# The end of the second layer of a two-layer selective-scan kernel: earlier loads, spread norm sums and a hand-ordered tail

## The chip, the cores and the metric

The kernel runs on one core of one Trainium2 chip. The metric is the device time of one execution in microseconds (us); lower is better. Of the kernel before the change three runs are shown, and their median is 1526.66 us (1522.29 to 1531.98).

## What is computed

Two layers work on an image x of 64 x 64 positions with 96 channels. Each adds a block to x: a group norm, a projection to 192 channels and 192 gate channels, a 3 x 3 convolution per channel with SiLU, a selective scan over the positions in four directions, the sum y of the four results, a layer norm over the 192 channels, the product with SiLU of the gates, and a projection back to 96 channels. The change is in the last steps of layer 2:

```python
y = out_y[:, 0] + out_y[:, 1, :, ::-1] + out_y[:, 2][:, :, i1] + out_y[:, 3][:, :, i2]
...
mu = y.mean(-1, keepdims=True)
var = y.var(-1, keepdims=True)
y = (y - mu) * lax.rsqrt(var + LN_EPS) * ln_gamma + ln_beta
y = y * jax.nn.silu(z)
return y @ out_proj_w.T
```

## The kernel before

**Layout.** The 192 channels of half the positions each lie in three tiles `y[T]`, T = 0, 1, 2, of 128 partitions by 2048 columns: 64 partitions for one half of the positions, 64 for the other. The columns are worked on in four chunks c of 512. x itself lies transposed, `xT`, 96 partitions by 4096 positions; two half chunks h of 512 positions belong to each c. In DRAM lie x (`xs`) and the gates after SiLU (`szd`), both written earlier.

**The scans of layer 2** (`scans`, from L839) are 16 groups (direction and chunk) of 24 units. A unit is one block T and one pair m of states: ScalarE makes the decay `a`, TensorE the input `b`, VectorE scans them to `h` (two units cost one product `b<-b,du` and two scans), GpSimd multiplies by C (`hc`), TensorE sums into `ys`. The order on every engine is written out by hand: in unit j a loop issues stage_B or stage_t, a, b, r, s, k, y and c for units near j, and then the extra steps whose slot has come. The extra steps of a group's prelude prepare the next group; those of `early_norms` (L1180) run in the last group. They do the layer norm of chunks 3, 2 and 1, which are complete by then: per chunk three matmuls for the mean (`em`), a copy, three subtractions on GpSimd, three squares on ScalarE, three matmuls for the variance (`ev`), and the reciprocal root into `u[0]`. Chunk 0 is completed by the last group itself. In each chunk the three matmuls of a sum fall into one unit.

**Pools.** `pre` holds the scan's tiles that live once, `mn` those with several buffers; `tail` opens after both are closed, and its tiles take over their memory. A new tile waits for the last use of the tiles that it lies on. The memory is given out in the order in which tiles are first asked for. In the kernel before, `xT` (16 KB per partition) and the gate tiles `szt` lie on scan tiles up to the last group's `du`, `su` and `B3`.

**The tail of layer 2** (`tail`, L1490) has no fixed order; a scheduler orders each engine's instructions. All twelve gate tiles and four pieces of `xT` are loaded on SP's queue (L1505, L1507). `centre(0)` and `scale(0)` do the norm of chunk 0 (L1514 to L1529). Then for c = 3, 2, 1, 0: `gated` multiplies and shifts y and multiplies by the gates (L1538 and L1541 on VectorE; for T = 2 of chunks 3, 2 and 1 L1543 to L1545 on GpSimd and ScalarE), `project` does six matmuls into `o` (L1552) and two additions into `xT` (L1558), and `tokens` transposes back (L1569), copies (L1571) and sends the result (L1572), with a single PSUM buffer `t`.

Of the kernel before, what the change touches and what calls it, by code (L numbers as in the profile page):

```python
# [19 lines left out]
DM = 96  # L20
DI = 192
NS = 16
NP = NS // 2
RK = 6
TC = 1024
HT = TC // 2
NCH = L // TC
# [5 lines left out]
NB = 96  # L33
# [4 lines left out]
V_CW, V_CB, V_G, V_B, V_D = 0, 9, 10, 11, 12  # L38
NV = 16

HALF = (slice(0, 64), slice(64, 128))
# [3 lines left out]
def two_ss2d_layers(  # L45
# [46 lines left out]
    ident = const.tile([128, 128], F32, name="ident")  # L92
    make_identity(nc, ident)

    pos = const.tile([128, 128], F32, name="pos")
# [10 lines left out]
    for h in range(2):  # L106
        t = const.tile([128, 128], F32, name=f"wide{h}")
# [10 lines left out]
    eps5 = const.tile([128, 1], F32, name="eps5")  # L118
# [25 lines left out]

    u = [pers.tile([128, L // 2], F32, name=f"u{T}") for T in range(3)]
    y = [pers.tile([128, L // 2], F32, name=f"y{T}") for T in range(3)]
    xs = dpool.tile([DM, L], F32, name="xs")
    szd = [dpool.tile([3, 128, L // 2], F32, name=f"szd{l}") for l in range(2)]

# [2 lines left out]
    xT = xp.enter_context(tc.tile_pool(name="xT0", bufs=1)).tile([DM, L], F32, name="xT0")  # L152
    st = [pers.tile([DM, 8, 6], F32, name=f"st{l}") for l in range(2)]
    with tc.tile_pool(name="ld", bufs=8) as ld, tc.tile_pool(
        name="ldp", bufs=4, space=PSUM
# [682 lines left out]
    def scans(weights):  # L838
# [18 lines left out]
        with ExitStack() as sc:  # L857
# [2 lines left out]
            pps = sc.enter_context(tc.tile_pool(name="pps", bufs=1, space=PSUM, reuse_waits="tile"))  # L860
            dram = sc.enter_context(tc.tile_pool(name="dram", bufs=3, space=DRAM))
            am = []
            carry = pre.tile([128, 3, NP], F32, name="carry")
            PER = 3 * NP
            LAG = 3
            halves = [slice(0, HT), slice(HT, TC)]
# [1 line left out]

            xd = pre.tile([128, TC], F32, name="xd")
            dve.memset(xd[96:128], 1.0)  # L870

            def spare(name, tag="v"):

# [304 lines left out]
            def early_norms():  # L1178


                steps = []
                squares = [chunk(u[T], 0) for T in range(3)]
                for c, at, lead, end in ((3, 2, 0, 8), (2, 8, 2.1, 14), (1, 14, 10, 20)):
                    me, mean = {}, chunk(u[1], c)

                    def average(me, c, of, T, what):
                        if T == 0:
                            me[what] = spare(f"{what}{c}")
                        pe.matmul(me[what], pos, of[T], start=(T == 0), stop=(T == 2))

                    def keep(me, mean):
                        act.copy(mean, me["em"])

                    def centre(T, c, mean):
                        pool.tensor_sub(chunk(y[T], c), chunk(y[T], c), mean)

                    def square(T, c):
                        act.activation(squares[T], chunk(y[T], c), AF.Square)

                    def root(me, c):  # L1200
                        act.activation(chunk(u[0], c), me["ev"], AF.Ln, bias=eps5)
                        act.activation(chunk(u[0], c), chunk(u[0], c), AF.Exp, scale=-0.5)

                    of = [chunk(y[T], c) for T in range(3)]
                    for T in range(3):
                        steps += [
                            (lead + 0.35 * T, partial(average, me, c, of, T, "em")),
                            (at + 2 * T, partial(centre, T, c, mean)),
                            (at + 2 * T + 1.5, partial(square, T, c)),
                            (end + 0.35 * T, partial(average, me, c, squares, T, "ev")),  # L1210
                        ]
                    steps += [(lead + 1.1, partial(keep, me, mean)), (end + 1.4, partial(root, me, c))]
                return [(PER * (len(GROUPS) - 1) + at, step) for at, step in steps]

            units = [
# [274 lines left out]

    def tail(l, w, xT):


        op, v = w["op"], w["v"]
        with ExitStack() as sc:
# [14 lines left out]
            def centre(c):  # L1510
                cut = slice(HT * c, HT * (c + 1))
                pm = fps.tile([128, HT], F32, tag="m", name=f"m_{l}_{c}")
                for T in range(3):
                    nc.tensor.matmul(pm, pos, y[T][:, cut], start=(T == 0), stop=(T == 2))  # L1514
                for T in range(3):
                    nc.vector.tensor_sub(y[T][:, cut], y[T][:, cut], pm)
                    sq = live[c, T] = fin.tile([128, HT], F32, tag=f"sq{T}", name=f"sq{l}_{c}_{T}")
                    nc.scalar.activation(sq, y[T][:, cut], AF.Square)

            def scale(c):  # L1520
                cut = slice(HT * c, HT * (c + 1))
                pv = fps.tile([128, HT], F32, tag="v", name=f"v_{l}_{c}", bufs=1)
                for T in range(3):
                    nc.tensor.matmul(pv, pos, live[c, T], start=(T == 0), stop=(T == 2))
                rstd = live[c] = fin.tile([128, HT], F32, tag="rstd", name=f"rstd{l}_{c}")
                if c == order[0] and not l:
                    load_exp_ln()
                nc.scalar.activation(rstd, pv, AF.Ln, bias=eps5)
                nc.scalar.activation(rstd, rstd, AF.Exp, scale=-0.5)  # L1529

            def gated(c):
                cut = slice(HT * c, HT * (c + 1))
                rstd = live.pop(c) if c in live else u[0][:, cut]
                for T in range(3):
                    q = live[c, T] = fin.tile([128, HT], F32, tag=f"g{T}", name=f"g{l}_{c}_{T}")
                    gain, bias = v[:, T, V_G : V_G + 1], v[:, T, V_B : V_B + 1]
                    if l == 0 or T < 2 or c == 0:
                        nc.vector.scalar_tensor_tensor(  # L1538
                            q, y[T][:, cut], gain, rstd, ALU.mult, ALU.mult
                        )  # L1540
                        nc.vector.scalar_tensor_tensor(q, q, bias, sz[c, T], ALU.add, ALU.mult)  # L1541
                    else:
                        nc.gpsimd.tensor_mul(q, y[T][:, cut], rstd)  # L1543
                        nc.scalar.activation(q, q, AF.Identity, bias=bias, scale=gain)
                        nc.gpsimd.tensor_mul(q, q, sz[c, T])  # L1545

            def project(c):
                gs = [live.pop((c, T)) for T in range(3)]
                po = fps.tile([DM, 2, HT], F32, tag="o", name=f"o{l}_{c}")
                for T in range(3):  # L1550
                    for h, half in enumerate(HALF):
                        nc.tensor.matmul(  # L1552
                            po[:, h], op[half, T, :], gs[T][half], start=(T == 0), stop=(T == 2)
                        )
                for h in range(2):
                    g = 2 * c + h
                    cut = slice(g * 512, (g + 1) * 512)
                    nc.vector.tensor_add(xT[:, cut], po[:, h], xT[:, cut])  # L1558
                    if l == 0:
                        nc.vector.bn_stats(w["next"][:, g, :], xT[:, cut])  # L1560
                        nc.sync.dma_start(out=xs[:, cut], in_=xT[:, cut])

            def tokens(c):

                for g in (2 * c, 2 * c + 1):
                    pt = fps.tile([128, 4, DM], F32, tag="t", name=f"t{l}_{g}", bufs=1)
                    for j in range(4):
                        t = slice(g * 512 + 128 * j, g * 512 + 128 * (j + 1))
                        nc.tensor.transpose(pt[:, j], xT[:, t], ident[0:DM, 0:DM])  # L1569
                    ob = fin.tile([128, 4, DM], F32, tag="ob", name=f"ob{g}")  # L1570
                    nc.scalar.copy(ob, pt)  # L1571
                    nc.sync.dma_start(  # L1572
                        out=out[g * 512 : (g + 1) * 512, :].rearrange("(j p) c -> p j c", p=128),
                        in_=ob,
                    )

            if l:
                centre(0)
                scale(0)
                for c in order:  # L1580
                    gated(c)
                    project(c)
                    tokens(c)
                return
            steps = (centre, lambda c: (scale(c), gated(c)), project)
            for i in range(NCH + len(steps) - 1):
                for lag, step in enumerate(steps):
                    if 0 <= i - lag < NCH:
                        step(order[i - lag])

    for l in range(2):

# [108 lines left out]
```

## Time and profile before

| | us |
|---|---|
| median of three runs | 1526.66 |
| the profiled execution | 1525.39 |
| its span | 1523.6 |
| busy in the span: VectorE, TensorE, ScalarE, GpSimd | 1353.6, 1242.7, 1214.6, 1120.0 |
| last scan `h` ends | 1479.73 |
| first load of the tail issued | 1479.76 |
| last copy `ob` ends | 1520.05 |

Times in the profile are us from the start of the span. A timeline line gives start, busy time, engine, line, operation, what is written and read, and how many instructions are merged in it; in brackets stands the idle time of the engine ahead of it and what ended it. L852 is the line of the helper that records all instructions of the scans, so that there one goes by tile names. Of each 512-column fp32 matmul the trace holds two records. `SPq` is the sequencer that issues DMAs.

### The profile page before, as it was taken

Reading aid. Unit: us, or ns where it says so; the run is one execution under the profiler, and the core shown is the slowest. Engines: PE = TensorE matmul, PEld = TensorE weight load, DVE = VectorE, ACT = ScalarE, POOL = GpSimd, SP = SyncE. Lnnn points to the kernel's source line nnn. Section 1 sums busy time; section 2 is a strip of 40 time slices with the busy share of each in tenths; the row PEclk is TensorE's granted clock in tenths of the full one; section 3 lists DMA queues with packets and bytes.
Section 4 is the critical chain, followed back from the end, with each engine's and each line's share of the span. In section 5 each row is a group of like instructions: output and inputs, shape, how many; then the busy total and the mean of one; then the engine's idle time right before and its main releaser. Section 6 shows DMA issues by size and latency. Waiting matters only on the chain.

```text
span 1523.6 us, 17338 instructions
## 1 busy us (share of the span) xinstructions
PE 1242.7 (82%) x5122; PEld 499.9 (33%) x5122; DVE 1353.6 (89%) x945; ACT 1214.6 (80%) x2498; POOL 1120.0 (74%) x608
## 2 busy tenths in 40 slices
PE   6944879688788888889788888797988888876986
PEld 3323433233232323333333333333333233322332
DVE  5956579579999999999999999999999999999985
ACT  6573355679998989898999889989898989887852
POOL 0023000369999898989898989898989899899991
PEclk9965889579998999999999999999989998999998
DMA  3230512514352626162626262626353444535324
GB/s 110 78 88 2 136 42 83 126 30 111 85 133 64 147 62 154 56 140 56 140 57 139 58 139 60 149 68 141 75 122 86 110 101 94 121 75 132 77 59 134
DMA packets 79796, 146.33 MB, mean 96 GB/s; under 512 B 27676, under 2 KB 30940, under 8 KB 79596
## 3 DMA queue, kind: packets, MB, share of 16 engines
q1 hardware_dynamic: 78540, 142.78, 38.7%
q0 software_dynamic: 576, 1.57, 0.4%
q8 instruction: 42, 0.69, 0.2%
q10 hardware_dynamic: 576, 0.79, 0.2%
q14 instruction: 62, 0.51, 0.1%
HBM read 80.85 MB, written 12.13 MB: 61 GB/s over the span
## 4 chain that ended last, share of the span: by engine, by line
DVE 29%; issue 21%; PE 13%; ACT 8%; DMA 6%; POOL 6%; SPq 5%; DVEq 0%; POOLq 0%; ACTq 0%
DVE h L852 16%; DVE b L852 7%; POOL hc L852 4%; SPq L852 4%; PE ys L852 4%; DMA cb<-C 3%; ACT a L852 3%; DVE acc L1468 3%; PE b L852 3%; PE pj L852 2%; ACT bT L852 2%; DMA du<-su 2%; DMA szt<-szd 2%; PE pd L852 1%; PE o L1552 1%
## 5 line engine op out<-in xcount | busy, mean ns | idle before, releaser
L852 POOL TENSOR_TENSOR hc<-h,cb 128x1024 f32<-128x1024 f32 x384 | 903.2, 2367 | 109.0 <-DVE h L852 60.2
L852 DVE TENSOR_TENSOR_SCAN h<-a,carry,b 128x1024 f32<-128x1024 f32 x288 | 664.9, 2337 | 30.1 <-PE b L852 7.2
L852 ACT ACTIVATE a<-dt,am 128x1024 f32<-128x1024 f32 x384 | 438.5, 1142 | 92.6 <-DVE h L852 87.4
L852 PE MATMUL ys<-hc,fold 128*64 128x512 f32 x1536 | 430.1, 640 | 2.8 <-POOL hc L852 2.8
L852 ACT ACTIVATE bT<-duT,BT 128x192 f32<-128x192 f32 x1012 | 386.9, 445 | 6.5 <-PE b L852 4.5
L852 PE MATMUL b<-ident,bT 128*128 128x128 f32 x1536 | 223.3, 289 | 30.7 <-DVE h L852 24.2
L852 DVE TENSOR_TENSOR b<-b,du 128x1024 f32<-128x1024 f32 x192 | 232.3, 1210 | 14.8 <-PE b L852 14.6
L852 DVE TENSOR_TENSOR_SCAN h<-a,b 128x1024 f32<-128x1024 f32 x96 | 216.0, 2277 | 15.1 <-PE b L852 4.5
L852 PEld LDWEIGHTS b<-ident,bT 128*128 128x128 f32 x1536 | 176.2, 147 | 156.6 <-DVE h L852 91.5
L852 PE MATMUL b<-B,selh 96*128 96x512 bf16 x384 | 122.7, 403 | 84.2 <-DVE h L852 84.2
L852 PEld LDWEIGHTS ys<-hc,fold 128*64 128x64 f32 x1536 | 78.4, 139 | 139.8 <-issue 98.5
L852 PE MATMUL pj<-u,xw 64*124 64x512 f32 x192 | 97.9, 656 | 5.2 <-ACT sz L1425 2.0
L852 PE MATMUL pd<-xd,dwb 29*64 29x512 f32 x192 | 61.1, 714 | 47.8 <-DVE w L852 41.1
L852 PEld LDWEIGHTS <-selh 96*128 96x128 bf16 x384 | 26.4, 98 | 213.8 <-DVE h L852 114.5
L1468 DVE SCALAR_TENSOR_TENSOR acc<-pad,v,acc 128x1052 f32<-128x1052 f32 (+1 forms) x80 | 91.3, 1200 | 0.6
L852 POOL DMA_DIRECT2D du<-su x12 | 6.4, 538 | 83.0 <-DVE am L237 80.5
L852 PE MATMUL ys<-y,ident 128*128 128x512 f32 (+1 forms) x120 | 63.0, 631 | 0.0
L852 ACT CAST B<-pj 96x512 bf16<-96x512 f32 (+2 forms) x96 | 54.9, 575 | 4.8 <-PE pj L852 4.8
L852 POOL TENSOR_TENSOR sp<-sp,ln 128x512 f32<-128x512 f32 x45 | 57.5, 1278 | 0.2
L852 POOL TENSOR_TENSOR su<-sp,u 128x512 f32<-128x512 f32 x45 | 57.5, 1278 | 0.0
L852 POOL TENSOR_TENSOR ln<-ln,w 128x512 f32<-128x512 f32 x45 | 57.5, 1277 | 0.0
L852 PEld LDWEIGHTS pj<-u,xw 64*124 64x124 f32 x192 | 34.6, 196 | 65.4 <-issue 45.0
(177 smaller groups left out, 1200.1 us busy)
## 6 DMA issues: line engine op xcount, KB each, us to landing
cb<-C SPq DMA_DIRECT2D x256, 256.0 KB
dt<-sp SPq DMA_DIRECT2D x192, 128.0 KB
du<-su SPq DMA_DIRECT2D x180, 128.0 KB
szd<-sz SPq DMA_DIRECT2D x24, 256.0 KB
szt<-szd SPq DMA_DIRECT2D x24, 256.0 KB
xT<-xs SPq DMA_DIRECT2D x8, 384.0 KB
xs<-xT SPq DMA_DIRECT2D x1, 1536.0 KB
xs<-xT SPq DMA_DIRECT2D x8, 192.0 KB
```

What stands on the lines that cost most here:

```text
L852: return lambda *args, **more: tc.keep_in_program_order(op(*args, **more))
L1468: nc.vector.scalar_tensor_tensor(acc, src, wk, acc, ALU.mult, ALU.add)
L1552: nc.tensor.matmul(po[:, h], op[half, T, :], gs[T][half], start=(T == 0), stop=(T == 2))
```

## The change

Four things change, all in layer 2.

- **Tiles that are free early come first.** `carry` moves to another pool, and `pre` asks first for the tiles that the last group's products no longer read late (`w`, `ln`, `turn`, `sp`, `su`, `BT`, `duT`, `B3`), so that the tail's `xT` and gate tiles lie on them.
- **Norm sums.** The matmuls of one sum stand in three units, one in each, where they stood in one; the steps after them have new slots.
- **The tail of layer 2 is a function of its own**, `last_tail`, in an order written by hand. Its loads stand ahead of everything else in it: gates of chunk 3, `xT` of chunk 3, and so on.
- **All gating is on VectorE**, one copy `ob` of eight goes from ScalarE to VectorE, and the transposes have two PSUM buffers.

In the program as built the first two gate tiles wait for TensorE's reads of `su` (ahead of the last group), the third for ScalarE's last `bT`, the first of chunk 1 for TensorE's last `b<-B`, and the last of chunk 0 for a product with `du`. No load waits for a scan any more. Some tiles of the start of layer 2's scans lie elsewhere too and wait for other tiles of the convolution.

```diff
+    carry = pers.tile([128, 3, NP], F32, name="carry")
...
-            carry = pre.tile([128, 3, NP], F32, name="carry")
...
+            room = [(nm, [128, HT], F32, 1) for nm in ("w", "ln")]
+            room += [("turn", [128, HT // 2], F32, 1)]
+            room += [(f"{nm}{T}", [128, HT], F32, 1) for nm in ("sp", "su") for T in range(3)]
+            room += [("BT", [128, 8, NS], F32, 2)]
+            room += [(f"duT{e}", [128, 2, 3, 64], F32, 1) for e in range(4)]
+            room += [("B3", [NB, TC], BF16, 3)]
+            for tag, shape, kind, bufs in room:
+                pre.tile(shape, kind, tag=tag, name=f"{tag}room", bufs=bufs)
...
-                for c, at, lead, end in ((3, 2, 0, 8), (2, 8, 2.1, 14), (1, 14, 10, 20)):
+                for c, lead, at, end in ((3, 0, 3, 9), (2, 4, 9, 15), (1, 12, 15, 21)):
...
-                            (lead + 0.35 * T, partial(average, me, c, of, T, "em")),
+                            (lead + T, partial(average, me, c, of, T, "em")),
                             (at + 2 * T, partial(centre, T, c, mean)),
-                            (at + 2 * T + 1.5, partial(square, T, c)),
-                            (end + 0.35 * T, partial(average, me, c, squares, T, "ev")),
+                            (at + 2 * T + 1, partial(square, T, c)),
+                            (end + T, partial(average, me, c, squares, T, "ev")),
                         ]
-                    steps += [(lead + 1.1, partial(keep, me, mean)), (end + 1.4, partial(root, me, c))]
+                    steps += [(lead + 2.5, partial(keep, me, mean)), (end + 2.5, partial(root, me, c))]
...
+            for c in order:
+                for T in blocks:
+                    sp.dma_start(out=sz[c, T], in_=szd[1][T, :, cut(c)])
+                xc = slice(TC * c, TC * (c + 1))
+                sp.dma_start(out=xT[:, xc], in_=xs[:, xc])
...
+            def average(of, name):
+                ps = live[name] = fps.tile([128, HT], F32, tag=name, name=f"{name}_0")
+                for T in blocks:
+                    pe.matmul(ps, pos, of[T], start=(T == 0), stop=(T == 2))
...
+            def gated(c, T):
+                q = live["g", c, T] = fin.tile(
+                    [128, HT], F32, tag=f"g{T}", name=f"g{c}_{T}", bufs=2
+                )
+                rstd = u[0][:, cut(c)] if c else live["rstd"]
+                dve.scalar_tensor_tensor(
+                    q, y[T][:, cut(c)], v[:, T, V_G : V_G + 1], rstd, ALU.mult, ALU.mult
+                )
+                dve.scalar_tensor_tensor(q, q, v[:, T, V_B : V_B + 1], sz[c, T], ALU.add, ALU.mult)
...
+                (dve.tensor_copy if g == 1 else act.copy)(ob, live["t", g])
...
+            for T in blocks:
+                gated(3, T)
+            gated(2, 0)
+            average([y[T][:, cut(0)] for T in blocks], "m")
+            centre()
+            project(3)
+            average([live["sq", T] for T in blocks], "v")
+            root()
+            for T in (1, 2):
+                gated(2, T)
+            project(2)
+            both_of(3)
+            tokens(3)
+            for T in blocks:
+                gated(1, T)
+            project(1)
+            both_of(2)
+            tokens(2)
+            for T in blocks:
+                gated(0, T)
+            both_of(1)
+            project(0)
+            tokens(1)
+            both_of(0)
+            tokens(0)
```

`centre`, `root`, `project`, `add` and `tokens` of the new function hold the same instructions as L1516 to L1572, each in program order; `both_of(c)` is the two additions of a chunk, and `tokens(c)` all eight transposes of the chunk and then its two copies and sends.

More of the change, by code (lines that the diff above doesn't have):

```diff
@@ L1491, in tail @@
     def tail(l, w, xT):
+        if l:
+            return last_tail(w, xT)
         op, v = w["op"], w["v"]
@@ L1525, in scale @@
                 rstd = live[c] = fin.tile([128, HT], F32, tag="rstd", name=f"rstd{l}_{c}")
-                if c == order[0] and not l:
+                if c == order[0]:
                     load_exp_ln()
@@ L1532, in gated @@
                 cut = slice(HT * c, HT * (c + 1))
-                rstd = live.pop(c) if c in live else u[0][:, cut]
+                rstd = live.pop(c)
                 for T in range(3):
@@ L1536, in gated @@
                     gain, bias = v[:, T, V_G : V_G + 1], v[:, T, V_B : V_B + 1]
[L1537 to L1545, printed above, removed]
+                    nc.vector.scalar_tensor_tensor(
+                        q, y[T][:, cut], gain, rstd, ALU.mult, ALU.mult
+                    )
+                    nc.vector.scalar_tensor_tensor(q, q, bias, sz[c, T], ALU.add, ALU.mult)
             def project(c):
@@ L1558, in project @@
                     nc.vector.tensor_add(xT[:, cut], po[:, h], xT[:, cut])
[L1559 to L1584, printed above, removed]
+                    nc.vector.bn_stats(w["next"][:, g, :], xT[:, cut])
+                    nc.sync.dma_start(out=xs[:, cut], in_=xT[:, cut])
             steps = (centre, lambda c: (scale(c), gated(c)), project)
@@ L1589, in tail, with last_tail, cut, centre @@
                         step(order[i - lag])
+    def last_tail(w, xT):
+        op, v = w["op"], w["v"]
+        with ExitStack() as sc:
+            fin = sc.enter_context(tc.tile_pool(name="fin1", bufs=1, reuse_waits="tile"))
+            fps = sc.enter_context(tc.tile_pool(name="fps1", bufs=1, space=PSUM, reuse_waits="tile"))
+            order = range(NCH - 1, -1, -1)
+            blocks = range(3)
+            sz, live = {}, {}
+            def cut(c):
+                return slice(HT * c, HT * (c + 1))
+            for c in order:
+                for T in blocks:
+                    sz[c, T] = fin.tile([128, HT], F32, tag=f"sz{c}{T}", name=f"szt{c}_{T}")
+            for c in order:
+                for T in blocks:
[6 more added lines that the diff above has]
+                    pe.matmul(ps, pos, of[T], start=(T == 0), stop=(T == 2))
+            def centre():
+                for T in blocks:
+                    dve.tensor_sub(y[T][:, cut(0)], y[T][:, cut(0)], live["m"])
+                    sq = live["sq", T] = fin.tile([128, HT], F32, tag=f"sq{T}", name=f"sq{T}")
+                    act.activation(sq, y[T][:, cut(0)], AF.Square)
+            def root():
+                rstd = live["rstd"] = fin.tile([128, HT], F32, tag="rstd", name="rstd")
+                act.activation(rstd, live["v"], AF.Ln, bias=eps5)
+                act.activation(rstd, rstd, AF.Exp, scale=-0.5)
+            def gated(c, T):
[5 more added lines that the diff above has]
+                    q, y[T][:, cut(c)], v[:, T, V_G : V_G + 1], rstd, ALU.mult, ALU.mult
+                )
+                dve.scalar_tensor_tensor(q, q, v[:, T, V_B : V_B + 1], sz[c, T], ALU.add, ALU.mult)
+            def project(c):
+                po = live["o", c] = fps.tile([DM, 2, HT], F32, tag="o", name=f"o{c}", bufs=2)
+                for T in blocks:
+                    for h, half in enumerate(HALF):
+                        pe.matmul(
+                            po[:, h], op[half, T, :], live["g", c, T][half],
+                            start=(T == 0), stop=(T == 2),
+                        )
+            def add(c, h):
+                s = slice(HT * (2 * c + h), HT * (2 * c + h + 1))
+                dve.tensor_add(xT[:, s], live["o", c][:, h], xT[:, s])
+            def turn(c, h):
+                g = 2 * c + h
+                pt = live["t", g] = fps.tile([128, 4, DM], F32, tag="t", name=f"t{g}", bufs=2)
+                for j in range(4):
+                    t = slice(g * HT + 128 * j, g * HT + 128 * (j + 1))
+                    pe.transpose(pt[:, j], xT[:, t], ident[0:DM, 0:DM])
+            def send(c, h):
+                g = 2 * c + h
+                ob = fin.tile([128, 4, DM], F32, tag="ob", name=f"ob{g}", bufs=3)
+                (dve.tensor_copy if g == 1 else act.copy)(ob, live["t", g])
+                sp.dma_start(
+                    out=out[g * HT : (g + 1) * HT, :].rearrange("(j p) c -> p j c", p=128), in_=ob
+                )
+            def tokens(c):
+                for h in range(2):
+                    turn(c, h)
+                for h in range(2):
+                    send(c, h)
+            def both_of(c):
+                for h in range(2):
+                    add(c, h)
+            for T in blocks:
+                gated(3, T)
[10 more added lines that the diff above has]
+            tokens(3)
+            for T in blocks:
+                gated(1, T)
+            project(1)
+            both_of(2)
+            tokens(2)
+            for T in blocks:
+                gated(0, T)
[4 more added lines that the diff above has]
+            tokens(0)
```

## The prediction

> **What bounds the kernel now.** I began with the page's slices, where VectorE is full until the last one and a half.
>
> ```profile
> DVE  5956579579999999999999999999999999999985
> PEclk9965889579998999999999999999989998999998
> ```
>
> All the change touches lies in the last 120 us, and the scans ahead of it keep their instructions. I read those by engine. First the timeline of VectorE: here the rhythm of a pair of units (starts of `b<-b,du` 5.84 us apart) and its one break.
>
> ```profile
> 1466.67 1.21 DVE L852 TENSOR_TENSOR b<-b,du 128x1024 f32<-128x1024 f32 x1
> 1468.01 4.58 DVE L852 TENSOR_TENSOR_SCAN h<-a,carry,b 128x1024 f32<-128x1024 f32 x2
> 1473.78 1.23 DVE L852 TENSOR_TENSOR b<-b,du 128x1024 f32<-128x1024 f32 x1 [1.19 <-PE b L852]
> 1475.14 4.59 DVE L852 TENSOR_TENSOR_SCAN h<-a,carry,b 128x1024 f32<-128x1024 f32 x2
> 1481.25 1.59 DVE L1538 SCALAR_TENSOR_TENSOR g<-y,v,u 128x512 f32<-128x512 f32 x1 [1.52 <-PE ys L852]
> 1483.56 6.82 DVE L1538 SCALAR_TENSOR_TENSOR g<-y,v,u 128x512 f32<-128x512 f32 x5 [0.71 <-PE ys L852]
> 1490.30 1.87 DVE L1516 TENSOR_TENSOR y<-y,m 128x512 f32<-128x512 f32 x3
> 1492.10 5.06 DVE L1541 SCALAR_TENSOR_TENSOR g<-g,v,szt 128x512 f32<-128x512 f32 x6
> 1498.60 1.48 DVE L1538 SCALAR_TENSOR_TENSOR g<-y,v,rstd 128x512 f32<-128x512 f32 x2 [1.44 <-ACT rstd L1529]
> ...
> 1507.50 1.29 DVE L1558 TENSOR_TENSOR xT<-o,xT 96x512 f32<-96x512 f32 x2 [3.45 <-PE o L1552]
> 1512.26 1.28 DVE L1558 TENSOR_TENSOR xT<-o,xT 96x512 f32<-96x512 f32 x2 [3.47 <-PE o L1552]
> 1517.01 1.28 DVE L1558 TENSOR_TENSOR xT<-o,xT 96x512 f32<-96x512 f32 x2 [3.47 <-PE o L1552]
> ```
>
> The last scan ends at 1479.73 (call that S). The tail takes 43.9 us from there to 1523.6. Until 1498 VectorE does first halves of gating while it lacks the gates, then TensorE sets the pace: chunks follow 4.75 us apart. Second, SP's queue and its waits:
>
> ```profile
> 1408.87 53.66 SPq L852 DMA_DIRECT2D cb<-C  x14
> 1479.76 0.78 SPq L1507 DMA_DIRECT2D xT<-xs  x2
> 1480.64 5.67 SPq L1505 DMA_DIRECT2D szt<-szd  x9
> ```
> ```profile
> SPq L1507 <- DVE h L852: 17.2, 1, 17.2
> ```
>
> The queue is free at 1462.5 and waits 17.2 us for the last scan. Third, TensorE's timeline:
>
> ```profile
> 1470.46 2.84 PE L852 MATMUL ev<-u,pos 128*128 128x512 f32 x6
> 1483.36 2.84 PE L1514 MATMUL m<-y,pos 128*128 128x512 f32 x6
> 1491.69 5.49 PE L1524 MATMUL v<-sq,pos 128*128 128x512 f32 x6 [5.49 <-ACT sq L1518]
> ```
>
> The `ev` burst stands ahead of `b` and makes VectorE's 1.19 us break. `v` takes 5.49 us for what `m` did in 2.84: granted clock 0.5, after 5.5 us of idleness.
>
> **The Trainium skill.** "GPSIMD Engine Reference", 1. Specifications, says that GpSimd shares its SBUF interfaces with VectorE instructions that have two SBUF inputs. The trace agrees: gating `g<-y,v,u` has a median of 1.69 us beside GpSimd, 0.74 without. "TensorE: Matmul & The Clock Gate", HAM oscillation, warns of TensorE idling over about 3.4 us: `v` agrees, but 1478 to 1482 (1.58 us busy in 4) brought no drop in `m`. "DMA: Bandwidth & Descriptors", Queues, rings and completion order, says descriptors on one ring are consumed in order; so the last `cb`, issued before the loads, isn't held by them. The tail's loads before all come after the scans, so no run here shows that.
>
> **The change, part by part.**
>
> *Loads.* None is added. The sixteen (4.6 MB) now follow the last `cb` at about 1462.5. Issuing takes 0.32 to 0.47 us each; before they went at 292 GB/s between 1480 and 1492, so about 16 us. Chunks 3 and 2 wait only for uses finished by then; chunk 1 waits for the last `b<-B` (1473.7 before), so chunks 1 and 0 land by about 1482, and are wanted from S+14. Queued behind them are only the output sends. The scans cover the loading. If transfers slow them: gating beside a DMA share of 1.0 took 5.06/6 = 0.84 us against 0.74, 13%; on some 12 us of scanning that bounds the cost at 0 to 1.5 us. I take 0, since scans have one length, 2.32 us, throughout.
>
> *Norm sums.* The same 18 matmuls move; `ev` no longer stands ahead of the last `b`. Gain: that 1.19 us; pair spacings elsewhere in the group exceed 5.84 by 0.3 in all. GpSimd is full here (36.00 of 36 us from 1430 to 1466), its nine subtractions (1.27 us) start a unit later, and the last one could hold up a last `hc` by 1.3. Bounds -1.5 to +1.3; I take -1.2, because GpSimd had 2.45 us idle twice after them. S becomes 1478.5.
>
> *Start of layer 2's scans.* Moved tiles wait for earlier convolution work (its last gate matmul was over by 262; the first `du` went at 282): 0, and I see no cost if that cover went, for the same TensorE queue orders it.
>
> *Tail.* VectorE runs in written order. Counting from S, with 0.74 per gating and 0.03 of issue:
> - Eight gatings (chunk 3, block 0 of chunk 2). The last `hc` ended at S+2.56. GpSimd's product with gating beside it took 1.76 against 1.28, so I stretch it to S+3.4 (between 2.56 and that is open). Until then VectorE does some 2.1 gatings, 5.9 follow: S+7.9.
> - `ys` 1.08 and `m` 2.84 after `hc` are done at S+7.3, so the three subtractions start unhindered: 1.87, S+9.8.
> - Four gatings 3.1, S+12.9; additions of chunk 3, 1.28, S+14.2.
> - Six gatings 4.6, S+18.8; additions 1.28, S+20.1; six more, S+24.7; additions of chunk 1, S+26.0.
> - TensorE: sixteen records of `o<-g,op` took 3.89 us at 1497, eight pairs 0.43 apart (the two half chunks run side by side) and 0.45 to drain; so the last two pairs end `o` of chunk 0 1.3 us after its last gating, at S+26.0, and the additions run to S+27.3.
> - Transposes 0.55, copy 0.48, and from the last copy's end to the span's end 3.55 as before (1520.05 to 1523.6): S+31.9.
>
> TensorE's own sum at full clock: `m` and `v` 5.7, four projections of 3.0 (six pairs of 0.43 and 0.45), transposes 8 x 0.55: 22.1 of some 24 us. Its deadlines hold: projection 3 ends S+10.3 (wanted S+12.9), `v` S+13.1, root 1.3 later, S+14.4 (wanted S+20.1), projection 2 S+16.1 (wanted S+18.8). The second PSUM buffer, and the copy on VectorE (0.48), cost nothing: ScalarE is nearly idle. GpSimd's six products and ScalarE's three gatings go; VectorE gets six, 4.6 us, counted above.
>
> Sum: 43.9 becomes 31.9, -12.0, and -1.2 in the group: -13.2. The span becomes 1510.4. The profiled execution, 1525.39, lies 1.3 under the median, so from 1526.66 I get **1513.5**.
>
> **Rivals.**
> 1. *Slow clock in the first part.* TensorE is little busy from 1477.5 on. If it starts cold, `m` costs 2.65 more and VectorE, free at S+7.9, waits 2 us; later sums may add 1: 1516.5. For: clock 0.5 around 1468, 1492 and 1505. Against: `m` was at full clock after the same lull.
> 2. *Gates still late.* If the second gating finds no gates till 1488 (first use before at 1488.6), nothing can pass it: that is S+9.5 instead of S+2: +7.5, 1521. Against: the built waits all end by 1474.
> 3. *Cold tail, slower than before.* TensorE at half clock throughout: `ys` 1.84, two sums 10.98, four projections 20.6 (at 1504 eight records took 3.43, so twelve 5.15), transposes 4.4 to 8.8, all after S+2.6, then copy and end 4.0: S+44.4 to S+48.8. With -1.2 in the group that is -0.7 to +3.7: about 1528. It takes over when about 85% of this work is cold. Against: the clock recovered within 6 us each time.
> 4. *Little change in the group, or loads slow it*: +2, 1515.5.
>
> **How the numbers follow.** The forecast 0.60, own range 1509 to 1517.5; slow first part 0.22; late gates 0.06; cold tail 0.03; group 0.09. The three runs spread 1522 to 1532, so a median has some 3 us of doubt; range 1507.5 to 1520.5. VectorE's work bounds the gain: even without contention and waits the tail needs S+29.8 or so, -15.3. About 1% is what a measurement can tell from no change, and it lies at 1511.4: a third of the forecast's 0.60 lies below it, a tenth of the slow part's and a fifth of the group's: faster 0.25; slower needs 1542, which only a cold tail with a mishap reaches, 0.02; same 0.73.
>
> **What would show it.** Loads issued by 1474 and no wait for `szt` on VectorE; no `PE b` wait of 1.2 us near 1473; first gatings near 1.7 us, then 0.74; `m` and `v` 2.84 each; additions without 3.4 us waits; 31.9 us from last scan to end. A VectorE wait for `o` or `m`, or `v` at 5.5, speaks for the clock. Wrong altogether: a span within 5 us of before.

## The result and the profile after

The changed kernel took 1508.51 us (median of four runs, 1507.62 to 1512.13) against 1525.24 of the kernel before on the same chip (four runs; the three shown ahead had 1526.66): a ratio of 0.9891, 95% interval 0.9859 to 0.9923. Measured again in nine runs on another occasion it took 1512.57 against 1523.34: 0.9926 (0.99 to 0.9952). The forecast was -13.2 us, a ratio of 0.9914, which lies in both intervals. The profiled execution took 1508.21 us, its span 1506.2.

The page's slices show VectorE full up to the last one:

```profile
DVE  5966479579999999999999999999999999999998
PEclk9965789579999999999999999999999999999999
```

VectorE's timeline (start, busy time, and so on, as before; L853 and L261 are now the lines of the recording helpers):

```profile
1469.27 4.58 DVE L853 TENSOR_TENSOR_SCAN h<-a,carry,b 128x1024 f32<-128x1024 f32 x2
1473.78 0.90 DVE L261 SCALAR_TENSOR_TENSOR g<-y,v,u 128x512 f32<-128x512 f32 x1
1474.71 2.72 DVE L261 SCALAR_TENSOR_TENSOR g<-g,v,szt 128x512 f32<-128x512 f32 x1
...
1481.69 1.88 DVE L261 TENSOR_TENSOR y<-y,m 128x512 f32<-128x512 f32 x3
...
1486.39 1.28 DVE L261 TENSOR_TENSOR xT<-o,xT 96x512 f32<-96x512 f32 x2
...
1497.46 2.57 DVE L261 TENSOR_TENSOR xT<-o,xT 96x512 f32<-96x512 f32 x4
1502.10 0.56 DVE L261 COPY ob<-t 128x384 f32<-128x384 f32 x1 [2.06 <-DMA out_dram<-ob]
```

The last scan ends at S = 1473.85, and the tail lasts 32.35 us from there, where it lasted 43.87. No addition `xT<-o,xT` waits for `o` any more. The one wait of the tail is new: the last copy waits 2.06 us for a send that still reads its buffer. SP's queue issues the loads before the last scan ends. They stand behind the last `cb`, and among them the queue waits 3.4 us for TensorE's `b` (the second fence: us in total, times, longest) and 1.3 us for an earlier load of `xT`:

```profile
1404.42 53.65 SPq L853 DMA_DIRECT2D cb<-C  x14
1458.11 1.53 SPq L261 DMA_DIRECT2D szt<-szd  x3
...
1471.18 0.32 SPq L261 DMA_DIRECT2D xT<-xs  x1
```
```profile
SPq L261 <- PE b L853: 3.4, 1, 3.4
```

TensorE's timeline has both sums at full clock, 2.84 us each, where `v` took 5.49:

```profile
1477.94 2.84 PE L261 MATMUL m<-y,pos 128*128 128x512 f32 x6
1480.72 2.82 PE L261 MATMUL o<-g,op 64*96 64x512 f32 x12
1483.47 2.84 PE L261 MATMUL v<-sq,pos 128*128 128x512 f32 x6
```

For the comparisons I cut every profiled span into four parts: up to the first scan of layer 2's groups, groups 0 to 14, the last group (first scan's start to last scan's end S), and the tail (S to the span's end), all in us. Each ratio is against runs of the kernel before on the same chip and occasion.

| profile | to first scan | groups 0-14 | last group | tail | ratio of the runs, interval |
|---|---|---|---|---|---|
| before | 299.6 | 1109.7 | 70.45 | 43.87 | |
| after | 301.1 | 1103.9 | 68.84 | 32.35 | 0.9891 (0.9859-0.9923) |
| changed kernel again | 298.9 | 1105.1 | 68.84 | 32.36 | 0.9926 (0.99-0.9952) |
| old layout | 301.4 | 1107.4 | 68.83 | 32.24 | 0.9919 (0.9887-0.995) |
| old norm slots | 299.9 | 1105.8 | 70.55 | 33.06 | 0.9945 (0.9926-0.9963) |
| eight `ob` | 301.0 | 1117.6 | 68.84 | 31.65 | 0.9908 (0.988-0.9935) |
| new layout alone | 300.8 | 1104.9 | 69.15 | 46.43 | 1.0025 (1.0002-1.0049) |
| gating back on GpSimd | 300.2 | 1117.5 | 68.83 | 34.76 | 0.9935 (0.9909-0.9961) |
| VectorE gating, old order | 300.0 | 1107.4 | 70.45 | 40.89 | 0.9984 (0.9967-1.0001) |
| direct tokens | 301.6 | 1115.3 | 68.84 | 33.41 | 0.9935 (0.9912-0.9957) |
| one `t` | 299.1 | 1116.2 | 68.84 | 33.13 | 0.9928 (0.9908-0.9949) |
| old order, two `t` | 300.6 | 1116.3 | 69.16 | 40.92 | 0.9981 (0.9965-0.9996) |

From before to after the tail gives -11.5 us, the last group -1.6, the start +1.5 and groups 0 to 14 -5.8: -17.4 in the span. Groups 0 to 14 hold the same instructions in all twelve, yet differ by 13.7 us. The five long ones (1115.3 to 1117.6) belong to the profiles with the lowest mean granted TensorE clock, 0.906 to 0.911; the other seven had 0.913 to 0.918. Among these seven the four with the new layout (1103.9 to 1105.8) lie below the three with the old one (1107.4 to 1109.7), so the profiles don't exclude that the layout shortens the scans a little, the rival P of the expectations below. The medians don't show it: the old layout took 1510.62 us and the changed kernel 1512.57 on the same occasion. The -5.8 and the start's +1.5 are therefore no effect that this change is shown to have.

### The profile page after: what moved, and what is told of

It reads as the page before. It is cut to its first block, busy times and chain, and to the rows that moved or that the text cites. A ratio compares the mean times of both kernels' runs of the same rounds, so it can differ in the third digit from the quotient of the medians.

```text
span 1506.2 us, 17332 instructions
## 1 busy us (share of the span) xinstructions
PE 1231.6 (82%) x5122; PEld 495.3 (33%) x5122; DVE 1354.9 (90%) x952; ACT 1212.6 (81%) x2494; POOL 1111.2 (74%) x602
## 4 chain that ended last, share of the span: by engine, by line
DVE 29%; issue 20%; PE 11%; ACT 9%; POOL 8%; DMA 6%; SPq 4%; DVEq 0%; POOLq 0%; ACTq 0%
DVE h L853 16%; DVE b L853 7%; POOL hc L853 6%; SPq L853 4%; PE ys L853 4%; ACT a L853 4%; DVE acc L1477 3%; ACT bT L853 3%; DMA cb<-C 3%; PE pj L853 3%; PE b L853 2%; PE pd L853 1%; DMA szt<-szd 1%; DMA dt<-sp 1%; POOL ln L853 1%
## 5 line engine op out<-in xcount | busy, mean ns | idle before, releaser
L853 POOL TENSOR_TENSOR hc<-h,cb 128x1024 f32<-128x1024 f32 x384 | 903.6, 2371 | 101.6 <-DVE h L853 49.6
L853 DVE TENSOR_TENSOR_SCAN h<-a,carry,b 128x1024 f32<-128x1024 f32 x288 | 665.0, 2337 | 27.4 <-PE b L853 8.2
L853 ACT ACTIVATE a<-dt,am 128x1024 f32<-128x1024 f32 x384 | 438.3, 1142 | 71.9 <-DVE h L853 66.3
L853 PE MATMUL ys<-hc,fold 128*64 128x512 f32 x1536 | 431.2, 641 | 1.6 <-POOL hc L853 1.6
L853 ACT ACTIVATE bT<-duT,BT 128x192 f32<-128x192 f32 x1012 | 387.3, 445 | 8.4 <-PE b L853 6.5
L853 PE MATMUL b<-ident,bT 128*128 128x128 f32 x1536 | 220.2, 287 | 31.6 <-DVE h L853 25.1
L853 DVE TENSOR_TENSOR b<-b,du 128x1024 f32<-128x1024 f32 x192 | 232.1, 1209 | 11.1 <-PE b L853 11.0
L853 DVE TENSOR_TENSOR_SCAN h<-a,b 128x1024 f32<-128x1024 f32 x96 | 216.0, 2277 | 14.4 <-PE b L853 6.5
L853 PEld LDWEIGHTS b<-ident,bT 128*128 128x128 f32 x1536 | 175.3, 146 | 155.2 <-DVE h L853 90.2
L853 PE MATMUL b<-B,selh 96*128 96x512 bf16 x384 | 120.9, 398 | 82.3 <-DVE h L853 82.3
L853 PEld LDWEIGHTS ys<-hc,fold 128*64 128x64 f32 x1536 | 78.3, 139 | 138.2 <-issue 100.6
L853 PE MATMUL pj<-u,xw 64*124 64x512 f32 x192 | 98.1, 657 | 5.2 <-ACT sz L1434 2.0
L853 PE MATMUL pd<-xd,dwb 29*64 29x512 f32 x192 | 58.4, 684 | 48.6 <-DVE w L853 41.8
L853 PEld LDWEIGHTS <-selh 96*128 96x128 bf16 x384 | 26.2, 98 | 209.4 <-DVE h L853 113.2
L853 POOL DMA_DIRECT2D du<-su x12 | 6.4, 536 | 82.7 <-ACT am L235 80.5
L853 PE MATMUL ys<-y,ident 128*128 128x512 f32 (+1 forms) x120 | 62.6, 627 | 0.0
L853 ACT CAST B<-pj 96x512 bf16<-96x512 f32 (+2 forms) x96 | 54.9, 575 | 4.7 <-PE pj L853 4.7
L853 POOL TENSOR_TENSOR ln<-ln,w 128x512 f32<-128x512 f32 x45 | 57.6, 1280 | 0.0
L853 POOL TENSOR_TENSOR sp<-sp,ln 128x512 f32<-128x512 f32 x45 | 57.5, 1277 | 0.2
L853 POOL TENSOR_TENSOR su<-sp,u 128x512 f32<-128x512 f32 x45 | 57.5, 1278 | 0.0
L853 PEld LDWEIGHTS pj<-u,xw 64*124 64x124 f32 x192 | 34.7, 196 | 65.4 <-issue 44.8
```

Of the source, the lines that this page charges most:

```text
L853: return lambda *args, **more: tc.keep_in_program_order(op(*args, **more))
```

## The experiments

**The changed kernel again**, unedited, to see how far a pair of profiles can be trusted.

> The changed kernel once more, unedited, as the base of the next three. In the first profile 11.5 us of the gain lay after the last scan, 1.7 us in the last group, and 4.2 us in groups 0 to 14, which the change doesn't edit. Theory A (the 4.2 us are chance: TensorE's clock and the spacing of units vary from run to run): the start of the last group moves by some us from profile to profile, and the gain over before is about 13 us with an uncertainty of 3. Rival P (the new places of the tiles make the scans faster): again some 17 us, and the last group starts at about 1416 us in this profile too.

Tail and last group agree with the first profile to 0.01 us; the medians differ from before by 10.8 us instead of 16.7. So where TensorE's clock runs alike, the tail and the last group can be read to a few hundredths from one profile, and the total to some 5 us only. The kernel before was profiled once. (The expectations date the start of the last group some 11 us later than the table's marks do, which put it at 1409.3 before and 1405.0 after. In this profile it is 1404.0.)

**Old layout**, new order: does the order need the early memory?

```diff
-    carry = pers.tile([128, 3, NP], F32, name="carry")
...
+            carry = pre.tile([128, 3, NP], F32, name="carry")
...
-            room = [(nm, [128, HT], F32, 1) for nm in ("w", "ln")]
...
-            for tag, shape, kind, bufs in room:
-                pre.tile(shape, kind, tag=tag, name=f"{tag}room", bufs=bufs)
```

> The changed kernel with the old places of the tiles (no tiles asked for early, carry back among them): the first load of x and all behind it wait for the last scan again, only the gates of chunk 3 come before. Theory A (the written order is what gains, and it asks for chunk 2's gates only 7 us after the last scan, when they have landed): 0 to 1.5 us slower than the changed kernel, no wait of VectorE for gates over 1 us. Rival L (loading during the last group is the lever): 5 us or more slower, with VectorE waiting for gates or x. Rival P on groups 0 to 14: the last group starts at about 1420 us as before, where A leaves it anywhere from 1414 to 1424.

SP's queue and VectorE, two timelines of this kernel, in which S is 1477.56:

```profile
1461.88 3.29 SPq L260 DMA_DIRECT2D szt<-szd  x3
...
1477.96 1.37 SPq L260 DMA_DIRECT2D szt<-szd  x3
```
```profile
1484.74 0.75 DVE L260 SCALAR_TENSOR_TENSOR g<-g,v,szt 128x512 f32<-128x512 f32 x1
```

The gates of chunk 3 are early even here; all that stands behind them is issued after S, as before. The first gating with a gate of chunk 2 starts 7.2 us after S and doesn't wait: chunk 3's gating stands ahead of it. The tail takes 32.24. The layout is worth nothing that shows beside the written order. What it would cost if chunk 3's gates were late as well wasn't tried.

**New layout alone**, put into the kernel before (the same lines, the other way round).

> The kernel before with the new places of the tiles alone: its tail keeps its order, its loads start during the last group. Counted from the last scan to the end of the profile (43.9 us before, 32.4 changed). Theory A (the loads weren't what held the old tail: VectorE worked on first halves meanwhile, and TensorE's cold sums and the order follow): 42 to 44 us. Rival L (late gates were the brake): 38 us or less.

The tail grew by 2.6 us, beyond both forecasts. The timelines of VectorE and GpSimd in this kernel, in which S is 1474.87:

```profile
1476.40 9.96 DVE L1547 SCALAR_TENSOR_TENSOR g<-y,v,u 128x512 f32<-128x512 f32 x6 [1.52 <-PE ys L853]
1486.28 1.87 DVE L1525 TENSOR_TENSOR y<-y,m 128x512 f32<-128x512 f32 x3
```
```profile
1477.40 5.07 POOL L1552 TENSOR_TENSOR g<-y,u 128x512 f32<-128x512 f32 x3
1482.42 5.05 POOL L1554 TENSOR_TENSOR g<-g,szt 128x512 f32<-128x512 f32 x3
```

GpSimd's second products no longer wait for gates and follow the first at once, beside VectorE's first gatings, which take 1.66 us each. So the subtractions start at S+11.4 (before: S+10.6), TensorE idles 6.32 us ahead of `v`, `v` takes 4.91 and ten records of a later projection 5.36. Earlier data fed contention. Of the 2.6 us, though, only 0.4 have come about by the first additions; 1.8 come between the additions, where the ten slow records fall, and 0.3 after the last. That the slow records follow from the earlier data isn't shown: the old order with two `t`, below, has ten of 5.26 us with late loads.

**Old norm slots** in the changed kernel.

```diff
-                for c, lead, at, end in ((3, 0, 3, 9), (2, 4, 9, 15), (1, 12, 15, 21)):
+                for c, at, lead, end in ((3, 2, 0, 8), (2, 8, 2.1, 14), (1, 14, 10, 20)):
...
-                            (lead + T, partial(average, me, c, of, T, "em")),
+                            (lead + 0.35 * T, partial(average, me, c, of, T, "em")),
...
-                            (end + T, partial(average, me, c, squares, T, "ev")),
+                            (end + 0.35 * T, partial(average, me, c, squares, T, "ev")),
                         ]
-                    steps += [(lead + 2.5, partial(keep, me, mean)), (end + 2.5, partial(root, me, c))]
+                    steps += [(lead + 1.1, partial(keep, me, mean)), (end + 1.4, partial(root, me, c))]
```

> The changed kernel with the norm matmuls of one sum in one unit again. Theory A: the wait of 1.2 us of VectorE for the input b near the end of the last group comes back, and the last group is 1 to 2 us longer (from the start of its first scan to the end of its last). Rival N (the burst was hidden, or its cost came only from a slow clock at that moment): under 0.5 us.

The last group grew by 1.7 us, but not at the `ev` burst that the prediction had named. Here are TensorE and VectorE of this kernel near the group's start:

```profile
1404.49 1.97 PE L853 MATMUL b<-ident,bT 128*128 128x128 f32 x8 [0.62 <-DVE h L853]
...
1407.91 2.84 PE L853 MATMUL em<-y,pos 128*128 128x512 f32 x6
```
```profile
1411.23 1.23 DVE L853 TENSOR_TENSOR b<-b,du 128x1024 f32<-128x1024 f32 x1 [0.95 <-PE b L853]
```

The eight `b` in front of the burst take 1.97 us instead of 1.09 (granted clock 0.50 from 1404.3 to 1406.4), and the pair comes 1.04 us late, the next 0.41. In the profile of before the same stands at the end, ahead of its `ev` burst:

```profile
1466.81 1.95 PE L852 MATMUL b<-ident,bT 128*128 128x128 f32 x8 [0.62 <-DVE h L852]
```

In the kernel with the old order and two `t`, below, which also has the old slots, TensorE is at full clock and its `ev` burst costs nothing:

```profile
1474.36 1.09 PE L852 MATMUL b<-ident,bT 128*128 128x128 f32 x8 [0.62 <-DVE h L852]
...
1476.39 2.84 PE L852 MATMUL ev<-u,pos 128*128 128x512 f32 x6
```

Its group takes 69.16, the one with the new layout alone 69.15. The changed kernel had its half clock in the same place as the one with old slots, eight `b` of 1.97 us at 1403.81, and all its pairs 5.84 or 5.85 apart. So a burst of three matmuls fits into its unit where the work ahead of it ran at full clock, and breaks the rhythm where that ran at half clock; spreading it is worth 0.3 us or 1.6 to 1.7, by where the clock falls. What makes it fall there stays open.

The tail of this kernel is 0.7 us longer than the changed kernel's. There too the clock was half for a while (0.50 from 1479.3 to 1482): `m` took 3.50 us, and VectorE waited for it.

```profile
1484.74 1.88 DVE L261 TENSOR_TENSOR y<-y,m 128x512 f32<-128x512 f32 x3 [0.59 <-PE m L261]
```

**Gating back on GpSimd**, new order kept: T = 2 of chunks 3, 2 and 1.

```diff
...
+                if T == 2 and c:
+                    pool.tensor_mul(q, y[T][:, cut(c)], rstd)
+                    act.activation(q, q, AF.Identity, bias=bias, scale=gain)
+                    pool.tensor_mul(q, q, sz[c, T])
+                else:
+                    dve.scalar_tensor_tensor(q, y[T][:, cut(c)], gain, rstd, ALU.mult, ALU.mult)
+                    dve.scalar_tensor_tensor(q, q, bias, sz[c, T], ALU.add, ALU.mult)
```

> The changed kernel, its order kept, with the gating of block 2 of chunks 3, 2 and 1 back on GpSimd and ScalarE. From the last scan to the end, changed 32.4 us. Theory A (GpSimd's two-input products slow VectorE's gating to less than half its speed while they run, which gives back what the six gatings saved): 32 to 36 us. Rival V (VectorE is the bound and only its own work counts): 28 to 31 us, 4.6 us of gating less.

The tail takes 34.76, 2.4 more than with all gating on VectorE. TensorE and VectorE:

```profile
1503.64 1.10 PE L261 MATMUL o<-g,op 64*96 64x512 f32 x4 [1.67 <-POOL g L261]
```
```profile
1490.04 1.75 DVE L261 SCALAR_TENSOR_TENSOR g<-y,v,u 128x512 f32<-128x512 f32 x1
```

VectorE has six instructions less, 4.4 us, and loses more: five gatings beside a GpSimd product take 1.63 to 1.75 instead of 0.75, and the projections wait for GpSimd's `g` (1.67, 1.25). The order, with the layout and the second `t`, still gives 9.1 of the 11.5 us.

**VectorE gating in the old order**: the kernel before with one condition changed.

```diff
-                    if l == 0 or T < 2 or c == 0:
+                    if True:
```

> The kernel before with all gating on VectorE and nothing else: the loads late, the order left to the scheduler. From the last scan to the end, before 43.9 us. Theory A (about half of the gain is the end of GpSimd beside the gating: the first halves take 0.74 for 1.69, the centring comes some 3 us earlier, and TensorE idles too short to go cold before the variance): 36 to 40 us. Rival O (the written order is all of it): 42 us or more.

The tail takes 40.89, 3.0 less, which lies between the two forecasts: five first gatings take 3.40 us instead of 6.82, and `v` 2.84. But the chunks still come 4.75 us apart, and the additions wait as they did. TensorE's timeline shows why:

```profile
1508.16 0.52 PE L1569 MATMUL t<-ident,xT 96*128 96x96 f32 x4
1508.62 1.10 PE L1552 MATMUL o<-g,op 64*96 64x512 f32 x2
1509.64 0.55 PE L1569 MATMUL t<-ident,xT 96*128 96x96 f32 x4
1510.13 1.96 PE L1552 MATMUL o<-g,op 64*96 64x512 f32 x8
```

The transposes `t` wait for the additions of their chunk, and in TensorE's queue ten of the twelve records of the next chunk's projection stand behind them; the next additions wait for that projection. It is a ring: additions, transposes, projection, additions.

**Old order with two `t`** asks whether the single PSUM buffer made that ring. It is the kernel just above, VectorE gating included, with a second buffer (the bank is taken from `m`). **One `t`** asks the same of the changed kernel.

```diff
-                pm = fps.tile([128, HT], F32, tag="m", name=f"m_{l}_{c}")
+                pm = fps.tile([128, HT], F32, tag="m", name=f"m_{l}_{c}", bufs=2 - l)
...
-                    pt = fps.tile([128, 4, DM], F32, tag="t", name=f"t{l}_{g}", bufs=1)
+                    pt = fps.tile([128, 4, DM], F32, tag="t", name=f"t{l}_{g}", bufs=2)
```

> The kernel before with all gating on VectorE and two PSUM buffers for the transposes (the bank comes from m, which has one use), the scheduler's order otherwise kept. If the order is what keeps the rhythm of 4.75 us (TensorE's transposes of a chunk and the additions stand in a ring with the next projection, whatever the buffers), the additions still wait 2.5 us and more for o and the tail stays at 39 to 41 us. Rival, the single buffer: the ring opens, the waits for o fall under 1.5 us, and the tail is 34 to 37 us.

```diff
-                pt = live["t", g] = fps.tile([128, 4, DM], F32, tag="t", name=f"t{g}", bufs=2)
+                pt = live["t", g] = fps.tile([128, 4, DM], F32, tag="t", name=f"t{g}", bufs=1)
```

> The changed kernel with one PSUM buffer for the transposes (t) where it has two. In its written order the transposes of a chunk stand behind the projection of the next one, and VectorE has six gatings (4.4 us) between two pairs of additions; one buffer makes the second four transposes wait for the copy of the first (0.5 to 1 us), which is then hidden except at the end, where the last four transposes would wait for one copy. If the order is what the gain is made of: tail 32.3 to 33.3 us, ratio within 0.002 of the changed kernel. Rival, that the second buffer is what broke the 4.75 us rhythm of the tail before: waits of 1 us and more for o come back between the additions and the tail grows by 3 us and more.

In the old order with two buffers the tail takes 40.92 us, as with one, and VectorE still waits twice:

```profile
1515.40 1.29 DVE L1558 TENSOR_TENSOR xT<-o,xT 96x512 f32<-96x512 f32 x2 [6.08 <-PE o L1552]
1520.81 1.28 DVE L1558 TENSOR_TENSOR xT<-o,xT 96x512 f32<-96x512 f32 x2 [4.12 <-PE o L1552]
```

The equal tails alone prove little, for a stretch of half clock fell into each: with one buffer (0.50 from 1496 to 1500) into the first of its three waits, which is gone here, with two into the wait of 6.08, where ten records took 5.26 us instead of 2.81. The last wait is the cleaner comparison: the clock was 1.00 from 1517 to 1521, and it is no shorter than the 3.47 with one buffer. So the second buffer didn't open the ring there.

In the changed kernel with one buffer the tail takes 33.13, 0.8 more, and that is at its end, where the last four groups of transposes come 1.16 us apart, each behind the copy before it. Between chunks nothing shows: there is no wait for `o`. So with a single buffer, too, the written order has no ring. `last_tail` puts the projection of a chunk ahead of the transposes of the chunk before it.

**Eight `ob`** in the changed kernel takes away what the last copy waited for.

```diff
-                ob = fin.tile([128, 4, DM], F32, tag="ob", name=f"ob{g}", bufs=3)
+                ob = fin.tile([128, 4, DM], F32, tag="ob", name=f"ob{g}", bufs=8)
```

> The changed kernel with eight buffers for the token tiles ob in place of three. In the changed kernel the very last copy, on VectorE, waits 2.06 us for the send of the fifth tile, whose buffer it takes. Theory A: that wait goes, the last copy ends about 0.6 us after the last transpose, and the time from last scan to end shortens by 1.2 to 1.6 us. Rival: the send of the tile before it ends the run anyway, under 0.4 us.

```profile
1514.31 0.56 DVE L261 COPY ob<-t 128x384 f32<-128x384 f32 x1 [0.77 <-PE t L261]
```

The copy waits only for its transposes and comes 1.3 us sooner after the additions; but from its end to the span's end it is now 4.13 us, not 3.54, and the tail is 0.7 us shorter, which lies between the two forecasts. Why the end takes longer stays open; it took 4.0 in the kernel with gating back on GpSimd, which has three `ob`. The ratio, 0.9908, can't be told from that of the changed kernel.

**Direct tokens**: TensorE makes the result in token layout (x by an identity product, the gated chunk as the stationary operand), without additions or transposes, with eight `ob` and six `t`. This kernel's result isn't the reference's; its time alone is read.

```diff
...
-                            po[:, h], op[half, T, :], live["g", c, T][half],
-                            start=(T == 0), stop=(T == 2),
...
+                                live["t", 2 * c + h][:, j],
+                                live["g", c, T][half, 128 * j : 128 * (j + 1)], op[half, T, :],
+                                start=False, stop=(T == 2), skip_group_check=True,
...
```

> The changed kernel with another end: TensorE makes the result in token layout at once (x by a product with the identity, then per block 64-row products with the gated tile as weights, all into one sum), so that the eight additions on VectorE and the transposes after them go; eight token buffers. From the last scan to the end, changed 32.4 us. Theory A (VectorE's 27 us of work are the bound, 5.1 of them the additions, and its last gating is then followed by some 1.5 us of TensorE, a copy and the send): 27.5 to 30 us. Rival T (the many small products with a weight load each make TensorE the bound): 32 us or more.

```profile
1511.42 2.92 PE L261 MATMUL t<-op,g 64*128 64x96 f32 x48
```
```profile
1514.48 0.56 DVE L261 COPY ob<-t 128x384 f32<-128x384 f32 x1 [6.98 <-PE t L261]
```

VectorE loses the additions, 5.1 us (8 by 0.64), and the tail grows to 33.41: a chunk now costs TensorE 4.8 us (1.92 for x and 2.92) where projection and transposes cost 3.7 (2.82 and 0.88). TensorE became the bound, at work without a gap from `m` to the end, and VectorE waits 6.98 us for the last chunk. So this way of taking work off VectorE asks more of TensorE than the tail has room for.

None of these versions beats the changed kernel by more than its interval.

## Why the prediction was right, and where not

The forecast's mechanism held: VectorE paces the tail without a gap up to the last additions, TensorE stays under it at full clock, and the cost is a sum over VectorE's instructions. Step by step, from S:

| step | predicted | measured |
|---|---|---|
| eight gatings over | 7.9 | 7.8 |
| three subtractions over | 9.8 | 9.7 |
| four gatings; additions of chunk 3 | 12.9; 14.2 | 12.5; 13.8 |
| six more; additions of chunk 2 | 18.8; 20.1 | 18.1; 19.3 |
| six more; all additions | 24.7; 27.3 | 23.6; 26.2 |
| last copy over | 28.35 | 28.8 |
| end of the span | 31.9 | 32.35 |

- **Gatings.** Two start 1.45 us apart, 0.72 each, where 0.77 was used; over the sixteen after the subtractions that is 0.8 us of the 1.1 gained by S+26.2. The first eight hit their sum, but not by the price of 1.69 us that the prediction gave to a gating beside GpSimd (3.4 us hold 2.0 of these, not 2.1): the first two took 0.90 and 2.72, and what the second waited for is told in the last section.
- **The last copy** is the term of the sum that was too small. From the end of the additions the prediction put transposes and copy at 1.03 us, and they took 2.6. The copy takes the buffer of the fifth `ob` of eight, for there are three buffers, and it waited 2.06 us until that tile was sent; 1.3 of these were left after its transposes, as the run with eight `ob` shows. That ate the 1.1 and 0.45 more. Before, the fifth copy and the last started 5.9 us apart and nothing waited; the new order brings them to 2.8. The prediction had looked at engines and PSUM, not at who still reads `ob`. The buffer is the same on either engine, so nothing shows that the copy's move to VectorE matters; the copy on ScalarE wasn't tried.
- **Norm sums**: -1.2 predicted, -1.6 measured. The reason given, a burst ahead of `b`, was right but half of it: the burst alone costs 0.3 us, and the rest needs TensorE at half clock ahead of it, which no step had asked for. One reading was wrong and had no effect: GpSimd was idle 0.91 and 2.45 us after its subtractions, not 2.45 twice.
- **Loads** at 0: right, and for a stronger reason than given. The 13% that the prediction held against them weren't theirs: of the six gatings in the 5.06 us five took 0.74 each, and the sixth took 1.75 beside a GpSimd product. Even issued after S, the thirteen loads behind chunk 3's gates were not waited for. Rival 2 priced gates late for the second gating at +7.5; it didn't come about and wasn't tried.
- **Start of layer 2's scans** at 0: the first scan lies at 298.9 to 301.6 in all twelve profiles, old and new layout mixed.
- **Clock** (rivals 1 and 3): `m` and `v` at 2.84 and twelve projection records at 2.82 (3.0 predicted) leave no room for either in this profile. Rival 1 came about in small in the kernel with the old norm slots, where the subtractions waited 0.59 us for `m`. The old order shows more of it: where additions and TensorE waited for each other, ten projection records took 5.26 or 5.36 in two profiles.
- **The size**: -13.2 predicted; tail and last group give -13.1. That it is so close is luck: work up to the last additions put too dear by 1.1 us and norm sums put 0.4 too small happened to cancel a last copy put too cheap by 1.55. The first medians gave -16.7 and the second -10.8. No profile goes with a median; between profiles, what differs so much are groups 0 to 14. About 3 us of doubt had been given to a median, and that is what was met.

## What to carry to other kernels

Look for rings in the order of a queue as well as in its buffers: put the work that the bound engine waits for next ahead of the work that waits for that engine. Feeding data earlier helps only where something waits for it, and it can hurt where it lets two engines contend at once. When an order is tightened, list for each instruction on the bound engine everything it waits for, its output buffer's last reader included.

## What the runs showed of the hardware

- The contention that the Trainium skill names ("GPSIMD Engine Reference", 1. Specifications) looks like waiting for a turn here, not like a slower rate. A gating takes 0.74 us alone. In the twelve profiles' tails 35 took 0.89 to 2.73, and each of them ended 0.55 us after the end of a GpSimd product that ran when it began or began with it. In the changed kernel the second of the two last `hc` ran from 1474.08 to 1476.88, and the gating that began beside it at 1474.71 ended at 1477.43:

```profile
1471.76 5.12 POOL L853 TENSOR_TENSOR hc<-h,cb 128x1024 f32<-128x1024 f32 x2 [0.74 <-DVE h L853]
```

- That `hc`, which began beside a gating itself, took 2.80 for 2.36. So what contention costs depends on when each starts: a median of 1.69 is no price for one gating.
- Groups 0 to 14 took 1103.9 to 1117.6 us in twelve profiles, the long ones where the mean granted clock of the profile was 0.911 or less. A single profile's span says little on a change of 10 us; its parts do.
- TensorE was at half clock with waits of 1.50 and 0.62 us just ahead (eight `b` of 1.97 us instead of 1.09 at 1403.81 in the changed kernel), at full clock in the same place in the kernel with the new layout alone.
- From the last copy's end to the span's end took 3.5 to 4.0 us in the ten profiles with three `ob`, 4.1 in the two with eight.
